# A late copy of row 0, a program order for POOL, k and x products in threes, and a first tile in quarters

## The chip, the cores and the metric

The kernel runs on one core of one Trainium2 chip. The metric is the device time in microseconds (us) of one execution; the time of a kernel is the median of eight executions.

## The reference, cut to what matters

The input x is 8 images of 256 channels of 96x96, in float32. Two residual layers follow each other, each on a group-normalised x (32 groups).

```
# layer 0: attention over channels on the 2D spectrum, 8 heads of 32 channels
q, k, v = [fft2(w @ gn(x) + b) for (w, b) in ((w1, b1), (w2, b2), (w3, b3))]
q, k    = q / norm(q), k / norm(k)                  # norms over all 96*96 frequencies
attn    = einsum('bhcn,bhdn->bhcd', q, k)
attn    = softmax(real(attn)) + 1j * softmax(imag(attn))
x       = x + w_out @ abs(ifft2(einsum('bhcd,bhdn->bhcn', attn, v)))
# layer 1: linear attention over positions; q and k have 32 rows, v has 256
q, k    = softplus(Wq @ gn(x) + bq), softplus(Wk @ gn(x) + bk)
v       = Wv @ gn(x) + bv
kv      = einsum('bdn,ben->bde', k, v)
x       = x + einsum('bnd,bde->ben', q, kv) / einsum('bnd,bd->bn', q, sum(k, over n) + 1e-6)
```

The kernel does no FFT of the image. It takes the attention from sums of products of an image with itself turned by 180 degrees, and from the turned image it makes the result in place.

## The kernel before, in words

An image is kept in SBUF as 128 partitions by 2 (the 256 channels) by 9216 columns. There are two such arenas; image b lies in one of them and its turned copy y in the other, which then takes the next image. A tile t is 8 rows of an image (12 tiles, loaded from t = 11 down to 0); `load_x` (L135) issues the loads of a tile on SP's queue, as two chunks of four rows.

Every image goes through five stages, each a Python generator:

- Pair sums (`pair_sums`, L325 on), 37 steps. A step takes 128 columns of x and the 128 opposite ones, which are turned back to the same order in `turn_back` (L364), one step ahead. In `turn_back`, at the first step of a tile, POOL first gathers the tile's column 0 in w0 (L371, L373 and, for t = 0, three smaller copies); then a copy from x, on POOL or ACT, writes the turned half to `back` (L387). PE transposes both halves in four matmuls each of 128x128 (L399, L400) into one PSUM tile, ACT scales and empties it into `xt` (L401), POOL (L414) or DVE (L416) form sum and difference in `eo`, and PE multiplies both with themselves into two accumulators (`products`, L333), one step later. From image 1 on the tiles t >= 5 are also spilled from xt to DRAM (L406, written xtd) for the next stage. Near the end of the stage the weights wl are loaded into a ring tile (L427).
- Attention (`attention`, L444 on): group norm, the covariances with the weights (L465), the softmax, with POOL's memsets L555 ahead of DVE's L558 and PE's product L561, and the matrix mz (POOL's memset L580).
- Rotation (`rotate`, L598 on): 48 steps of two rows each make the turned image y. `load_r` (L607) fetches a rotation matrix of six rows into a tm buffer, and POOL copies one column of it (L621). A step transposes two rows (PE L652, ACT L664) or fetches spilled ones from DRAM (L638, written xT<-xtd), and multiplies the rows of the step before last with tm (PE L655); DVE copies the result to ys (L660) and, turned, to y (L661). Row 0 has no partner and is copied as it is: POOL's copy L676 into y and memset L677 of ys, issued in the step where h is 0, step 6 of 48 (counted from 0). y lies in the arena of the image before, so its first writer waits until the outputs of that image have been stored.
- Images (`images`, L690 on): products with mz (L735), the squares and roots on DVE, ACT and POOL (L776 to L783), the product with w_out (L747), and x + result on DVE (L749). POOL sets two columns of the tiles of the next stage to 1.0 (L723).
- Layer 1 (`layer1`, L761 on) and its output (`output`, L949 on). Layer 1 works in 18 steps: PE transposes 512 columns of x in eight matmuls into two PSUM tiles (L893), ACT and DVE empty these into a slot (L896, L898), and `add_kx` (L871) multiplies a slot with the transposed k in eight matmuls with 32 columns of weights (L873). There are three slots. Two are in the constant tile xT and one is two tm buffers; a list `pend` holds the steps not yet multiplied, and products are issued for two steps together, just before the next step is appended. The softplus of k (DVE's L866 its last operation) and its transposes (PE L884, ACT L885) come once in three steps.

Buffers: psum has five rotating tiles for all transposes and products and three accumulators; the ring has four tiles of 128 x 1536 (xt, wl, own, e and others take turns); xT has six slots of 128 x 512, whose last two hold eo in the pair sums.

The stages are woven: `weave` advances one generator while another runs. The attention of image b runs beside its rotation; the pair sums of image b+1 run beside the images stage, layer 1 and output of image b. Where nothing else is said a scheduler orders each engine's instructions; within `tc.manual_schedule(engines=...)` the engines named keep the order in which the program issues them. That is PE around attention and rotation (L1025), and all five engines around the output stage (L1031 on), in which the generator of the next image's rotation is created but not yet run. POOL was free to be reordered in attention and rotation.

Of the kernel before, what the change touches and what calls it, by code (L numbers as in the profile page):

```python
# [62 lines left out]
TR = 6  # L63
# [9 lines left out]
def two_layer_kernel(ctx: ExitStack, tc: tile.TileContext, x, w1t, b1, w2t, b2, w3, b3, wot, temp,  # L73
                     wqt, bq, wkt, bk, wvt, bv, gavg, gmat, tmat, out):
    nc = tc.nc
    B, C, H, W = x.shape
    HW = H * W
    NT = H // ROWS
    TW = ROWS * W
    CH = 384  # L80
    PR = CH // W
# [18 lines left out]
    def x_of(b):  # L100
        return arenas[b % 2]
# [25 lines left out]
    def ring_tile(name):  # L127
        return ring.tile([P, 6 * C], F32, tag="ring", name=name)
# [5 lines left out]

    def load_x(b, t):  # L135
        loaded.add((b, t))
        for c in (2 * (NT - 1 - t), 2 * (NT - 1 - t) + 1):
            for h, n in chunk_rows(c):
                nc.sync.dma_start(out=x_of(b)[:, :, x_col(h):x_col(h) + n * W], in_=x_v[b, :, :, h * W:(h + n) * W])
# [185 lines left out]
    def pair_sums(b):  # L325
# [38 lines left out]
        def turn_back(i):  # L364

            t, j = steps[i]
            assert (b, t) in loaded
            if j == 0:
                col = x[:, :, (NT - 1 - t) * TW:(NT - t) * TW:W]
                h, o = PR * t, H // 2 + 1 + PR * t  # L370
                nc.gpsimd.tensor_copy(w0[:, :, h:h + PR], col[:, :, 0:PR])  # L371
                if t:
                    nc.gpsimd.tensor_copy(w0[:, :, o:o + PR], col[:, :, :PR - 1:-1])  # L373
                else:
                    nc.gpsimd.tensor_copy(w0[:, :, o:o + 1], col[:, :, 0:1])
                    nc.gpsimd.tensor_copy(w0[:, :, o + 1:o + PR], col[:, :, 2 * PR - 2:PR - 1:-1])
                    nc.gpsimd.tensor_copy(w0[:, :, o - 1:o], col[:, :, 2 * PR - 1:])
            if j == 0:
                xts.append(ring_tile(f"xt_{b}_{t}_{j}").rearrange("p (j c n) -> p j c n", j=3, c=2))
            ab = sides(t, j)  # L380
            ready = len(ab) == 1

            front = ab[0][2] if ready else xts[-1][:, j % 3, 0].rearrange("p (k n) -> p k n", k=KC)
            for p0, n, *v in ab:
                for c in range(ready, 2):
                    if v[c] is not None:
                        (nc.scalar.copy if b and t < T0 and (ready or not c) else nc.gpsimd.tensor_copy)(  # L387
                            (front, back[:, i % 2])[c][:, :, p0:p0 + n], v[c])
            return front, xts[-1][:, j % 3]

        steps = [(t, j) for t in range(NT - 1, -1, -1) for j in range(3)] + [(0, 3)]
# [206 lines left out]
    def rotate(b):  # L598

        y = image(y_of(b))  # L600
        ys = one.tile([P, KC, H + 1], F32, tag="ys", name=f"ys_{b}")

        def spilled(h):

            return b > 0 and PR * T0 <= h < H - PR * T0 and h != H // 2

        def load_r(h):  # L607
            tm = three.tile([P, TR * (W + 1)], F32, tag="tm", name=f"tm_{b}_{h}")[0:W].rearrange("p (r w) -> p r w", r=TR)
            turned = H // 2 <= h < H - PR * T0
            if b > turned:  # L610
                nc.sync.dma_start(out=tm, in_=rx[h // TR])
                return tm
            lo = 0
            while lo < TR:
                back = h + lo > H // 2 and spilled(h + lo)
                hi = lo + 2
                while hi < TR and back == (h + hi > H // 2 and spilled(h + hi)):
                    hi += 2
                nc.sync.dma_start(out=tm[:, lo:hi, 0:W], in_=window(h + lo, hi - lo, back))
                lo = hi  # L620
            nc.gpsimd.tensor_copy(tm[:, :, W:W + 1], csn[0:W, 2, h:h + TR].unsqueeze(2))  # L621
            if b == turned:
                nc.sync.dma_start(out=rx[h // TR], in_=tm)
            return tm


        pieces = [TR * i for i in (15, 4, 0, 5, 6, 14, 8, 3, 1, 7, 9, 13, 10, 12, 11, 2)]
        order = [h + r for h in pieces for r in range(0, TR, 2)]
        xts = {}

        def fetch(i):

            if i < len(order) and spilled(order[i]):
                xts[i] = xT[:, i % NX]
                h = order[i]
                c = h > H // 2
                rows = turned(c, H - h - 1 if c else h, 0)[0:2 * W]
                nc.sync.dma_start(out=xts[i][0:W, :, 0:C], in_=rows.rearrange("(r w) n -> w r n", w=W))  # L638

        def step(h, due, xt=None):  # L640

            if h is not None:
                pt = ps_tile(f"xr_{b}_{h}")
            if due is not None:
                g, gt, tm = due
                back = g > H // 2 and spilled(g)
                pu = ps_tile(f"y_{b}_{g}")
            for r in range(2):
                for k in range(KC):
                    if h is not None and h + r:  # L650
                        o = x_col(h + r)
                        nc.tensor.transpose(pt[0:W, r * C + k * P:r * C + (k + 1) * P], x_of(b)[:, k, o:o + W], ident)  # L652
                    if due is not None and g + r:
                        o = (r * KC + k) * (W + 1)
                        nc.tensor.matmul(pu[:, o:o + W + 1], lhsT=gt[0:W, 1 - r if back else r, k * P:(k + 1) * P], rhs=tm[:, g % TR + r, :],  # L655
                                         start=True, stop=True)
            if due is not None:
                src = pu[:, 0:2 * KC * (W + 1)].rearrange("p (r k w) -> p k w r", r=2, k=KC)
                r = 0 if g else 1
                nc.vector.tensor_copy(ys[:, :, g + r:g + 2], src[:, :, W, r:2])  # L660
                nc.vector.tensor_copy(y[:, :, :, g + r:g + 2], src[:, :, 0:W, r:2] if back else src[:, :, W - 1::-1, r:2])  # L661
            if h is not None:
                r = 0 if h else 1
                nc.scalar.copy(xt[0:W, r:2, 0:C], pt[0:W, r * C:2 * C].rearrange("p (r n) -> p r n", n=C))  # L664

        tms = [load_r(g) for g in pieces[0:3]]
        pieces = pieces[3:]
        pending = []
        for i, h in enumerate(order):
            if i % (TR // 2) == 0:  # L670
                tm = tms.pop(0)
            if i % (TR // 2) == 2 and i > 2 and pieces:
                tms.append(load_r(pieces.pop(0)))
            if h == 0:
                o = x_col(0)
                nc.gpsimd.tensor_copy(y[:, :, :, 0], x_of(b)[:, :, o:o + W])  # L676
                nc.gpsimd.memset(ys[:, :, 0:1], 0.0)  # L677
            if not spilled(h):
                xts[i] = xT[:, i % NX]
            step(None if spilled(h) else h, pending.pop(0) if len(pending) == 2 else None, xts[i])  # L680
            pending.append((h, xts.pop(i), tm))
            fetch(i + 3)
            yield
        for p in pending:
            step(None, p)
        y0[b] = ys
# [107 lines left out]
    def layer1(b):  # L794
# [78 lines left out]
                nc.tensor.matmul(kx[32 * j:32 * j + 32, 0:C + 1], lhsT=kT[:, 32 * j:32 * j + 32],  # L873
                                 rhs=xt[j // 2][:, j % 2, 0:C + 1], start=(i == 0), stop=(i == NS * CH // P - 1))

        slots = [*(xT[:, i] for i in range(4)), *kxt.pop(b)]
        pend = []
        softplus(0, 0)
        for s in range(NS):
# [4 lines left out]
                nc.tensor.transpose(pk[:, i * P:(i + 1) * P], kq(0, s)[:, i * P:(i + 1) * P], ident)  # L884
            nc.scalar.copy(kq(0, s), pk[:, 0:CH])  # L885
            for i in range(s * CH // P, (s + 1) * CH // P):
                xt = [slots[2 * (i % 3) + jj] for jj in range(2)]
                for jj in range(2):
                    pt = ps_tile(f"xT_{b}_{i}_{jj}")
                    for j in range(2):  # L890
                        o = (NB * s + 2 * jj + j) * CH + i % (CH // P) * P
                        for k in range(KC):
                            nc.tensor.transpose(pt[:, j * C + k * P:j * C + (k + 1) * P], x[:, k, o:o + P], ident)  # L893
                    src = pt.rearrange("p (j n) -> p j n", j=2)
                    if jj or i % 6 > 1:
                        nc.scalar.copy(xt[jj][:, :, 0:C], src)  # L896
                    else:
                        nc.vector.tensor_copy(xt[jj][:, :, 0:C], src)  # L898
                if s >= NS // 2 and i % (CH // P):
                    softplus(1, 2 * s - NS + i % (CH // P) - 1)  # L900
                if len(pend) == 2:
                    for p in pend:
                        add_kx(*p)
                    pend = []
                pend.append((i, xt, kq(0, s)[:, i % (CH // P) * P:(i % (CH // P) + 1) * P]))
                yield 0.25
# [115 lines left out]
        finish(sums)  # L1022
    turns = rotate(0)
    for b in range(B):
        with tc.manual_schedule(engines={mybir.EngineType.PE}):  # L1025
            weave(attention(b), turns)
            finish(turns)
        sums = pair_sums(b + 1) if b + 1 < B else iter(())
# [58 lines left out]
```

## Time and profile before

| | before |
|---|---|
| median of eight executions | 2731.66 us (2726.21 to 2749.8) |
| profiled execution | 2730.12 us |
| its span | 2728.3 us |
| mean granted clock of PE | 0.994 |
| PE's busy time | 2674.6 us (98%) |
| DVE, ACT, POOL | 1955.0, 1344.0, 884.8 us |
| HBM read, written | 151.25 MB, 118.06 MB |

The page gives the busy time of each engine over the span of one profiled execution, then the same in 40 slices of 68 us, with the granted clock of PE in tenths. The table of groups has one row for each line, engine and operation, with the mean duration of one instruction in ns and the idle time ahead of it, put down to the instruction that released it. The groups that the change touches:

```profile
L387 POOL COPY back<-arena 128x256 f32<-128x256 f32 (+1 forms) x230 | 89.6, 397 | 237.2 <-PE eoT L400 237.2
L400 PE MATMUL eoT<-ident,back 128*128 128x128 f32 x592 | 146.4, 274 | 1.8 <-POOL back L387 1.8
L676 POOL COPY arena<-arena 128x192 f32<-128x192 f32 x8 | 4.1, 510 | 25.4 <-DMA wl<-in_w_dram 11.8 <-DMA wl<-in_w2t_dram 6.5 <-DVE mv_a L295 3.4
L873 PE MATMUL kx<-xT,arena 128*32 128x257 f32 x768 | 56.3, 387 | 0.0
```

The timeline lists instructions by their start, with their duration, line, buffers and, in brackets, the idle time before them and who ended it.

### The profile page before, as it was taken

How to read it: one execution, taken by the hardware profiler on the slowest of the kernel's cores; microseconds unless marked ns; L12 is line 12 of the kernel's file. 1: busy time of each engine (PE TensorE's matmuls, PEld its weight loads, DVE VectorE, ACT ScalarE, POOL GpSimd, SP SyncE). 2: the span in 40 equal slices, each digit the busy share in tenths (PEclk: the TensorE clock that was granted, in tenths of full speed). 3: DMA queues.
4: the chain of work that ended last, by engine and by line, in shares of the span. 5: the costliest groups of instructions: out<-in, count | busy, mean ns of one | idle time of the engine just before them, and what ended most of it. 6: DMA issues, size and time to landing. Idle time of an engine off the chain costs nothing. (4 is left out here: it accounts for less than half of the span.)

```text
span 2728.3 us, 47818 instructions
## 1 busy us (share of the span) xinstructions
PE 2674.6 (98%) x17606; PEld 1915.0 (70%) x17606; DVE 1955.0 (72%) x4218; ACT 1344.0 (49%) x2125; POOL 884.8 (32%) x1334
## 2 busy tenths in 40 slices
PE   8999999999999999999999999999999999999987
PEld 8965678656785577956778566785677856778555
DVE  6678576875768767687666875768657687577776
ACT  3455653556525564255642556425564355643554
POOL 6133431334403334044340442404424134141311
PEclk9999999999999999999999999999999999999998
DMA  5220156202652026420364203641036311362003
GB/s 175 67 68 12 62 200 187 72 7 74 218 149 68 9 84 221 129 70 15 104 209 116 68 22 98 217 119 55 26 105 224 109 47 36 102 221 82 1 7 139
DMA packets 228635, 272.43 MB, mean 100 GB/s; under 512 B 34154, under 2 KB 216596, under 8 KB 228404
## 3 DMA queue, kind: packets, MB, share of 16 engines
q1 hardware_dynamic: 227460, 269.04, 31.3%
q8 instruction: 141, 2.31, 0.4%
q14 instruction: 90, 0.74, 0.1%
q10 hardware_dynamic: 944, 0.34, 0.0%
HBM read 151.25 MB, written 118.06 MB: 99 GB/s over the span
## 5 line engine op out<-in xcount | busy, mean ns | idle before, releaser
L735 PE MATMUL z<-arena,mz 128*128 128x384 f32 (+2 forms) x2400 | 595.0, 476 | 0.0
L747 PE MATMUL po<-e,wo 128*128 128x384 f32 x1536 | 529.8, 486 | 0.2 <-ACT e L782 0.2
L781 POOL TENSOR_TENSOR e<-e 128x768 f32<-128x768 f32 x192 | 348.6, 1816 | 554.0 <-ACT e L780 553.4
L735 PEld LDWEIGHTS z<-arena,mz 128*128 128x128 f32 (+1 forms) x2400 | 325.6, 163 | 241.4 <-issue 42.4
L333 PE MATMUL acc<-xT 128*128 128x256 f32 (+1 forms) x2368 | 449.1, 330 | 16.7 <-POOL xT L414 15.7
L747 PEld LDWEIGHTS po<-e,wo 128*128 128x128 f32 x1536 | 289.5, 190 | 197.7 <-DVE arena L749 1.2
L776 DVE TENSOR_TENSOR e<-z,xT 128x768 f32<-128x768 f32 x384 | 365.7, 952 | 85.2 <-PE z L735 85.1
L333 PEld LDWEIGHTS acc<-xT 128*128 128x128 f32 x2368 | 382.4, 191 | 60.2 <-POOL xT L414 21.2
L286 DVE BATCH_NORM_STATS2 st<-arena 128x6 f32<-128x384 f32 x768 | 409.7, 553 | 15.8 <-DMA arena<-in_x_dram 5.7
L655 PE MATMUL y<-tm,xT 96*128 96x97 f32 x3040 | 411.1, 269 | 1.6 <-DMA xT<-xtd 0.9
L655 PEld LDWEIGHTS y<-tm,xT 96*128 96x128 f32 x3040 | 402.1, 192 | 13.1 <-issue 7.4
L780 ACT ACTIVATE e<-e 128x1536 f32<-128x1536 f32 x192 | 284.5, 1482 | 91.4 <-DVE e L776 89.9
L782 ACT ACTIVATE e<-e 128x768 f32<-128x768 f32 x192 | 162.0, 844 | 336.7 <-POOL e L781 335.7
L401 ACT ACTIVATE xt<-eoT,pw 128x512 f32<-128x512 f32 x296 | 203.5, 687 | 163.7 <-PE eoT L400 153.7
L749 DVE TENSOR_TENSOR arena<-arena,po 128x384 f32<-128x384 f32 x384 | 211.0, 551 | 92.5 <-PE po L747 68.6
L414 POOL TENSOR_TENSOR xT<-xt 128x256 f32<-128x256 f32 x352 | 257.0, 747 | 60.4 <-ACT xt L401 59.3
L664 ACT COPY xT<-xr 96x512 f32<-96x512 f32 (+1 forms) x195 | 111.3, 574 | 276.4 <-PE xr L652 275.8
L661 DVE COPY arena<-y 128x384 f32<-128x384 f32 (+1 forms) x384 | 208.6, 546 | 2.0 <-issue 0.9
L652 PE MATMUL xr<-ident,arena 128*96 128x128 f32 x764 | 200.9, 279 | 0.0
L387 POOL COPY back<-arena 128x256 f32<-128x256 f32 (+1 forms) x230 | 89.6, 397 | 237.2 <-PE eoT L400 237.2
L988 DVE TENSOR_TENSOR arena<-arena,o 128x384 f32<-128x384 f32 x288 | 142.0, 549 | 33.8 <-PE o L983 33.8
L416 DVE SCALAR_TENSOR_TENSOR xT<-eoT,pw,xt 128x256 f32<-128x256 f32 x240 | 107.1, 478 | 81.9 <-ACT xt L401 81.9
(228 smaller groups left out, 3201.4 us busy)
## 6 DMA issues: line engine op xcount, KB each, us to landing
arena<-in_x_dram SPq DMA_DIRECT2D x184, 384.0 KB
out_dram<-arena SPq DMA_DIRECT2D x184, 384.0 KB
xT<-xtd SPq DMA_DIRECT2D x189, 192.0 KB
xtd<-xt SPq DMA_DIRECT2D x196, 128.0 KB
tm<-rx SPq DMA_DIRECT2D x107, 218.2 KB
xtd<-xt SPq DMA_DIRECT2D x98, 127.0 KB
rx<-tm SPq DMA_DIRECT2D x16, 218.2 KB
tm<-rt SPq DMA_DIRECT2D x16, 216.0 KB
```

The source lines that it names most:

```text
L286: nc.vector.bn_stats(out=st[:, k, c, :], in_=x_of(b)[:, k, c * CH:(c + 1) * CH])
L333: mm = nc.tensor.matmul(acc[c][:, m * C:m * C + (KC - m) * P], lhsT=t[0:np_, c, m * P:(m + 1) * P], rhs=t[0:np_, c, m * P:C], start=(first ...
L401: nc.scalar.activation(both, pt, AF.Copy, scale=pw[:, j:j + 1])
L414: on_pool(eo[:, c], both[:, 0], both[:, 1])
L655: nc.tensor.matmul(pu[:, o:o + W + 1], lhsT=gt[0:W, 1 - r if back else r, k * P:(k + 1) * P], rhs=tm[:, g % TR + r, :], start=True, stop=True)
L661: nc.vector.tensor_copy(y[:, :, :, g + r:g + 2], src[:, :, 0:W, r:2] if back else src[:, :, W - 1::-1, r:2])
L735: mm = nc.tensor.matmul(out[:, o:o + n * W], lhsT=columns(mz, k, c, j), rhs=y[:, k, h * W:(h + n) * W], start=(k == 0 and o == 0), stop=(k ...
L747: nc.tensor.matmul(po[:, 0:CH], lhsT=wo[:, k, m * P:(m + 1) * P], rhs=e[:, k, :], start=(k == 0), stop=(k == KC - 1))
L749: nc.vector.tensor_add(x[:, m, n], x[:, m, n], po[:, 0:CH])
L776: nc.vector.tensor_add(e[:, 2 * c:2 * c + 2, :].rearrange("p t (q h) -> p t q h", h=H), pz[:, 0:CH].rearrange("p (q h) -> p q h", h=H).uns ...
L780: nc.scalar.activation(e, e, AF.Square)
L781: nc.gpsimd.tensor_add(e[:, 0:2, :], e[:, 0:2, :], e[:, 2:4, :])
```

## The change

It has five edits.

1. `load_x`: the first tile of image 0 is loaded in four DMAs of two rows instead of two of four. The order of the rows is 44, 51, 46, 49 (the first row of each), so that opposite rows follow each other.
2. `turn_back`: the copies L387 are issued ahead of the copies of column 0 to w0 (L371 on).
3. `rotate`: row 0's copy and the memset of ys are issued at step 42 of 48 (counted from 0), right after the last rotation matrix has been fetched, instead of in the step where h is 0.
4. `layer1`: a fourth slot, `kring`, is taken from the ring, with a memset of its columns of 1.0 on POOL. Products are issued for three steps together.
5. The manual schedule around attention and rotation holds POOL as well as PE.

```diff
 def load_x(b, t):
     loaded.add((b, t))
+    if (b, t) == (0, NT - 1):
+        for h in (H // 2 - PR, H // 2 + PR - 1, H // 2 - 2, H // 2 + 1):
+            nc.sync.dma_start(out=x_of(b)[:, :, x_col(h):x_col(h) + 2 * W], in_=x_v[b, :, :, h * W:(h + 2) * W])
+        return
...
         if j == 0:
+            xts.append(ring_tile(f"xt_{b}_{t}_{j}").rearrange("p (j c n) -> p j c n", j=3, c=2))
+        ab = sides(t, j)
+        ready = len(ab) == 1
+
+        front = ab[0][2] if ready else xts[-1][:, j % 3, 0].rearrange("p (k n) -> p k n", k=KC)
+        for p0, n, *v in ab:
...
+        if j == 0:
             col = x[:, :, (NT - 1 - t) * TW:(NT - t) * TW:W]
...
-        if j == 0:
-            xts.append(ring_tile(f"xt_{b}_{t}_{j}").rearrange("p (j c n) -> p j c n", j=3, c=2))
-        ab = sides(t, j)
-        ready = len(ab) == 1
...
-        if h == 0:
+        if i == len(order) - TR:
             o = x_col(0)
             nc.gpsimd.tensor_copy(y[:, :, :, 0], x_of(b)[:, :, o:o + W])
             nc.gpsimd.memset(ys[:, :, 0:1], 0.0)
...
-    slots = [*(xT[:, i] for i in range(4)), *kxt.pop(b)]
+    kring = ring_tile(f"kx_{b}")[:, 0:4 * (C + 2)].rearrange("p (i j n) -> p i j n", i=2, j=2)
+    nc.gpsimd.memset(kring[:, :, :, C:C + 2], 1.0)
+    slots = [*(xT[:, i] for i in range(4)), *kxt.pop(b), *(kring[:, i] for i in range(2))]
...
-            xt = [slots[2 * (i % 3) + jj] for jj in range(2)]
+            xt = [slots[2 * (i % 4) + jj] for jj in range(2)]
...
-            if len(pend) == 2:
+            if len(pend) == 3:
...
-    with tc.manual_schedule(engines={mybir.EngineType.PE}):
+    with tc.manual_schedule(engines={mybir.EngineType.PE, mybir.EngineType.Pool}):
         weave(attention(b), turns)
         finish(turns)
```

More of the change, by code (lines that the diff above doesn't have):

```diff
@@ L368, in turn_back @@
             if j == 0:
+                xts.append(ring_tile(f"xt_{b}_{t}_{j}").rearrange("p (j c n) -> p j c n", j=3, c=2))
[3 more added lines that the diff above has]
+            for p0, n, *v in ab:
+                for c in range(ready, 2):
+                    if v[c] is not None:
+                        (nc.scalar.copy if b and t < T0 and (ready or not c) else nc.gpsimd.tensor_copy)(
+                            (front, back[:, i % 2])[c][:, :, p0:p0 + n], v[c])
+            if j == 0:
                 col = x[:, :, (NT - 1 - t) * TW:(NT - t) * TW:W]
@@ L377, in turn_back @@
                     nc.gpsimd.tensor_copy(w0[:, :, o - 1:o], col[:, :, 2 * PR - 1:])
-            if j == 0:
-                xts.append(ring_tile(f"xt_{b}_{t}_{j}").rearrange("p (j c n) -> p j c n", j=3, c=2))
-            ab = sides(t, j)
-            ready = len(ab) == 1
[L383 to L388, printed above, removed]
             return front, xts[-1][:, j % 3]
```

## The prediction

> **What bounds the kernel now.** I read the page's busy times and slices first, then who PE waited for, then the timelines at the longest of those waits.
>
> ```profile
> PE 2674.6 (98%) x17606; PEld 1915.0 (70%) x17606; DVE 1955.0 (72%) x4218; ACT 1344.0 (49%) x2125; POOL 884.8 (32%) x1334
> PE   8999999999999999999999999999999999999987
> PEclk9999999999999999999999999999999999999998
> ```
>
> PE is busy 98% of the 2728.3 us span, in every slice, at nearly full granted clock. So only two things shorten this kernel: removing PE's waits (some 54 us idle, plus what the clock loses after a wait), or making PE's own sequence cheaper. Time saved on POOL, DVE or ACT counts only where PE waits for it. The waits of PE:
>
> ```profile
> engine line waited for: us in total, times, longest us
> PE acc L333 <- POOL xT L414: 15.7, 14, 3.2
> PE kT L884 <- DVE arena L866: 6.2, 8, 3.6
> ```
>
> The first row is the largest: the pair-sum products L333 wait for POOL's subtraction L414. The timeline shows where, at the end of image 1's pair sums; POOL first, then PE:
>
> ```profile
> 414.85 0.73 POOL L414 TENSOR_TENSOR xT<-xt 128x256 f32<-128x256 f32 x1 [0.50 <-ACT xt L401]
> 415.51 0.10 POOL L677 MEMSET ys<- 128x2 f32 x1
> 419.23 0.51 POOL L676 COPY arena<-arena 128x192 f32<-128x192 f32 x1 [3.61 <-DMA wl<-in_w_dram]
> 419.61 0.72 POOL L414 TENSOR_TENSOR xT<-xt 128x256 f32<-128x256 f32 x1
> ```
>
> ```profile
> 415.82 2.43 PE L333 MATMUL acc<-xT 128*128 128x256 f32 x12
> 420.39 0.92 PE L333 MATMUL acc<-xT 128*128 128x256 f32 x4 [2.14 <-POOL xT L414]
> 421.15 1.04 PE L652 MATMUL xr<-ident,arena 128*96 128x128 f32 x8
> ```
>
> L414's input (ACT's L401) is ready at 416.76. It starts at 419.61 because row 0's copy L676 stands ahead of it on POOL and waits 3.61 us until the buffer it writes has been stored; the DMA named is merely the last to land by then. The same picture is there for images 1 to 7. Image 0's copy stands elsewhere (35.60) and PE does not wait for it.
>
> **What the Trainium skill says.** "PSUM — Partial Sum Buffer", section "Engine vs sequencer instructions", calls GpSimd's queue strict FIFO. The trace agrees: L414 with its input ready for 2.8 us stays behind L676. "TensorE: Matmul & The Clock Gate", section "What's actually happening", says that about 3.4 us of idle window bring half clock until a busy window has passed. The trace agrees in part: the granted clock is 0.50 in 757.8 to 761.2 and 1761.3 to 1764.7, right after two of these waits, though they last only 3.23 and 1.95 us. "TensorEngine Tiling (Array Packing)", section "Key Properties", says that changing the tiling mode drains TensorE; the kx products are 128x32 tiles between 128x128 transposes, and their cost at the change is measured below. "DMA: Bandwidth & Descriptors", section "Queues, rings and completion order", says that each DMA engine takes a ring's descriptors in order. The trace agrees: the first x tile's first half is there at 4.71, its second at 6.01.
>
> **Part 1: row 0's copy later, POOL in program order.** In the changed program's built order the copy and its memset stand behind the last of the copies L621 (image 0, 1) or the memset L580, after both last L414s. So in images 1 to 7 L414 follows L401: 416.76, plus 0.1 and 0.72, gives 417.6. PE finishes twelve products at 418.0 (415.82 plus eight and four at their usual pace, with 0.2 for DVE's L416), so no wait is left. Image 0 does the same sixteen in 73.22 to 76.14, 2.92 us. From the first to the transpose behind them, images 1 to 7 take 5.33, 6.42, 5.16, 4.83, 5.83, 5.12 and 4.42 us: 37.1, less 7 x 2.92 = 20.4, leaves **16.7**. The half clock also slows what follows: from that transpose to the qkm product (L465) it is 6.56 us in image 1, 8.18 in image 2 and 7.39 in image 5: **2.4** more. Sum 19.1.
>
> What is late next: DVE's first copy into that buffer (L661) waits for the same stores. It runs at 424.22; 2.4 earlier is 421.8, and L676 was released at 419.2, so 2.6 us of margin. The spilled rows (xT<-xtd) are issued from 417.16 on; their first product falls at about 425.5 now, 423.1 then, and the transfers queued before them drain at about 421.5 by the DMA packets: 1.5 us margin. The weights wl are needed only at 427.7.
>
> The copy itself, 0.51 us on POOL some six steps before the rotation ends, and the memset lie under PE's rotation; uncovered they would cost 8 x 0.6 = 5 us. Program order also puts the softmax memsets L555 behind some L621, which wait for PE to free a tm buffer; DVE's L558, then PE's L561, stand behind. Image 0 is the tightest: L558 at 116.58 moves behind the L621 of 117.63, about 1.5 us later; L561 comes at 126.24, so nothing reaches PE. L580 leaves the output stage, where POOL waited up to 4.9 us on it, but PE had no wait there: nothing.
>
> **Part 2: products of k and x for three steps together.** The timeline of PE around a group of two steps (each step is 8 records):
>
> ```profile
> 336.43 0.64 PE L873 MATMUL kx<-xt,arena 128*32 128x257 f32 x8
> 336.89 0.62 PE L873 MATMUL kx<-xT,arena 128*32 128x257 f32 x8
> 337.44 1.09 PE L893 MATMUL xT<-ident,arena 128*128 128x128 f32 x8
> 343.34 1.04 PE L893 MATMUL xT<-ident,arena 128*128 128x128 f32 x8
> 344.31 1.07 PE L873 MATMUL kx<-xT,arena 128*32 128x257 f32 x16
> 345.31 0.55 PE L884 MATMUL kT<-ident,arena 128*128 128x128 f32 x3
> ```
>
> Start to start, a step takes 0.46 inside a group and 0.55 as its last: leaving costs 0.09. Eight transposes take 0.97 before a group (343.34 to 344.31), against 0.87 elsewhere (332.85 to 333.72): entering costs 0.10. 18 steps in groups of three are six groups instead of nine: 3 x 0.19 = 0.57 us an image, 4.6 for eight. Against it: ahead of the first group PE now makes ten transposed tiles in a row instead of seven, through five PSUM buffers. Step 1's tiles are emptied at 331.84 by ACT and DVE; PE would want their buffers at about 331.6, so some 0.25 us an image goes back. Net 0.32 x 8 = **2.6**; bounds 4.6 gained and, if 0.15 us is lost at each of 48 groups, 2.6 lost.
>
> The fourth slot is a ring tile, so the pair sums have two tiles left beside it and own. The memset adds a wait on POOL: it needs xt_9's spill to have landed, and behind it are L414 of t = 7 and the products. That spill is issued by 311.8, the memset comes at about 325: nothing, as for the other tiles (xt_6 at 342.3 follows xt_8's spill, issued by 324.1; xt_5 at 364.6 that of xt_7, issued by 337.6). On SP, xt_6's last spill falls behind the tm loads, some 5 us later; xt_3, which takes its buffer, starts after 375.
>
> **Part 3: first tile in quarters, back copies first.** POOL's start now:
>
> ```profile
> 4.71 0.19 POOL L371 COPY w<-arena 128x8 f32<-128x8 f32 x1 [0.93 <-DMA arena<-in_x_dram]
> 6.01 0.19 POOL L373 COPY w<-arena 128x8 f32<-128x8 f32 x1 [1.10 <-DMA arena<-in_x_dram]
> 6.14 0.74 POOL L387 COPY back<-arena 128x256 f32<-128x256 f32 x2
> ```
>
> The first step needs the first two quarters, the bytes of the first half: at 4.7 instead of 6.0. POOL then copies back at once, and PE's first step ends about 1.4 us sooner. But the next step needs the last quarter, still near 6.0, and PE's fourth and fifth transposes need tile 10, which two more issues of 0.46 us on SP ahead of 23 loads push back. The trace has no transfer of this size, so bounds: 1.6 gained (the lead kept) to 0.5 lost (the issues dominate). I take **1.0**. In later images the copies L387 before L371 save POOL 0.4 us where PE does not wait.
>
> **Sum.** 19.1 + 2.6 + 1.0 = 22.7. The profiled execution took 2730.12 (span 2728.3 and 1.8 around it) and would take 2707.4; the median of the eight runs is 1.54 higher: 2731.66 - 22.7 = **2709.0**.
>
> **Rivals.** *Late rows* (0.12): PE reaches the spilled rows while stores, weights and they share the DMA engines. For: such a wait exists once (1.13 us at 477.8). Against: the 1.5 us margin. 7 x 1.1 = 7.7 back: 2716.7. *The wait moves* (0.05): DVE's L661 takes over L676's wait, so PE stops one step later and only 3.6 is gained: 2728.1. For: the same stores are awaited. Against: 2.6 us margin. *Slower* (0.05): PE waits for PSUM at each group of three, because ACT needs 5 x 0.59 + 0.48 + 0.62 = 4.1 us to empty what PE makes in 2.95. Without the 2.6, parts 1 and 3 give 20.1: it decides from 20.1/48 = 0.42 us a group. At 0.7 it costs 33.6, ending at 2745. Against: ACT is busy 26.1 of 35 us in this stage, and product blocks of 1.3 us lie between.
>
> **Chances and range.** The likeliest case has 0.78, 2709.0. Its own bounds: 2705 (all of part 2, 1.6 of part 3) to 2717 (part 2 losing, part 3 losing 0.5, and 1.3 of clock loss staying), with 4 us of run to run spread: 2700 to 2720, which takes in late rows. A measurement of this kernel tells about 0.3%, 8.2 us, from no change. Faster by more 0.90 (0.78 + 0.12), within 0.05, slower 0.05.
>
> **What would show it.** The row of L333 waiting for L414 falls from 15.7 to about 3; no half clock after the pair sums; kx records in runs of 24; PE's first L400 near 5.3 instead of 6.59. Wrong if y L655 waits for xT<-xtd in every image, if L661's idle grows, or if PE's transposes L893 wait for ACT's L896.

## The result, and the profile after

| | before | after |
|---|---|---|
| median | 2733.44 us (32 executions, 2725.89 to 2749.8) | 2719.39 us (11 executions, 2715.08 to 2723.72) |
| ratio after / before | | 0.9945, 95% interval 0.9929 to 0.9960 |
| profiled execution: span | 2728.3 us | 2716.3 us |

The kernel is 0.55% faster: 14.0 us by the medians, 10.9 to 19.4 by the interval. The forecast was 22.7 us. The line numbers of the changed kernel are 4 to 6 higher behind `load_x` (L414 is now L418, L676 is L680); in `turn_back`, turned round, L387 is now L381 and L371 is L386. First the page's busy times, PE's slices and its clock, after the change:

```profile
PE 2670.3 (98%) x17606; PEld 1911.7 (70%) x17606; DVE 1957.6 (72%) x4218; ACT 1342.6 (49%) x2125; POOL 884.0 (33%) x1342
PE   8999999999999999999999999999999999999987
PEclk9999999999999999999999999999999999999999
```

At this size nothing can be seen. The waits of PE show the difference (line, who is waited for, us in total, times, longest):

```profile
PE kT L890 <- DVE arena L870: 6.2, 8, 3.6
PE eoT L403 <- DMA arena<-in_x_dram: 5.2, 2, 3.9
PE xT L899 <- ACT xT L902: 2.8, 7, 0.4
PE zs L704 <- DVE ys L664: 2.8, 8, 0.3
PE acc L337 <- POOL xT L418: 1.8, 8, 0.3
```

The 15.7 us of the products on POOL's subtraction are 1.8. Two rows have come: the transposes of layer 1 wait for ACT's L902 once in seven of the eight images, and the first transposes wait a second time for x. The timeline of POOL at the end of image 1's pair sums, and later in its rotation:

```profile
417.06 0.74 POOL L418 TENSOR_TENSOR xT<-xt 128x256 f32<-128x256 f32 x1 [0.50 <-ACT xt L405]
419.11 0.73 POOL L418 TENSOR_TENSOR xT<-xt 128x256 f32<-128x256 f32 x1 [1.31 <-ACT xt L405]
...
472.36 0.19 POOL L625 COPY tm<-csn 96x6 f32<-96x6 f32 x1 [4.58 <-DMA xT<-xtd]
472.48 0.53 POOL L680 COPY arena<-arena 128x192 f32<-128x192 f32 x1
472.86 0.15 POOL L681 MEMSET ys<- 128x2 f32 x1
```

Nothing stands between the last two subtractions any more; POOL only waits for ACT, whose output it reads. Row 0's copy comes 53 us later and waits for nothing. PE at the same place and, further up in the same timeline, around layer 1's third group:

```profile
346.38 0.60 PE L899 MATMUL xT<-ident,arena 128*128 128x128 f32 x4
347.39 0.63 PE L899 MATMUL xT<-ident,arena 128*128 128x128 f32 x4 [0.41 <-ACT xT L902]
347.95 0.64 PE L877 MATMUL kx<-xt,arena 128*32 128x257 f32 x8
348.41 0.62 PE L877 MATMUL kx<-kx,arena 128*32 128x257 f32 x8
348.84 0.62 PE L877 MATMUL kx<-xT,arena 128*32 128x257 f32 x8
...
418.03 3.08 PE L337 MATMUL acc<-xT 128*128 128x256 f32 x16
420.95 1.04 PE L656 MATMUL xr<-ident,arena 128*96 128x128 f32 x8
```

The sixteen last products run through: 2.92 us from the first to the transpose behind them, where it was 5.33. The third group of kx products is now 24 records, and ahead of it PE stops for 0.41 us in the middle of a step's transposes.

To split the difference I cut the spans at starts of PE records: zs (L700), kT (L884) and den (L936) of each image, by the numbers of before. The way from den to the next zs holds the output, the end of the pair sums, attention and rotation; from kT to den lie the 18 steps of layer 1.

| stretch | before | after | difference |
|---|---|---|---|
| start to zs of image 0 | 150.25 | 152.05 | +1.80 |
| den to zs, images 1 to 7 | 825.42 | 808.17 | -17.25 |
| kT to den, images 0 to 6 | 273.76 | 276.46 | +2.70 |
| layer 1 of image 7 up to kT | 24.99 | 26.41 | +1.42 |
| den of image 7 to the end | 38.19 | 37.65 | -0.54 |

With the rest, -0.2, this is the 12.0 us between the spans. The 1.42 has no part of the change in it: after the same waits, PE's clock was granted at half for 6.8 us in the execution after and for 3.4 in the one before. Most of the 1.80 at the start is no part of the change either: PE's clock is full from 13.61 us on in the execution after, and from 10.28 in the one before. In the ten kernels below that load the first tile in halves, zs of image 0 comes about 0.5 us later for each us that the full clock comes later (10.28 and 150.25 us before, 13.11 and 151.69 in the last kernel of the table below); by this estimate 1.7 of the 1.80 are the clock's.

### The profile page after: what moved, and what is told of

Its sections match the earlier page's. It is cut to its first block, busy times and chain, and to the rows that moved or that the text cites. A ratio compares the mean times of both kernels' runs of the same rounds, so it can differ in the third digit from the quotient of the medians.

```text
span 2716.3 us, 47888 instructions
## 1 busy us (share of the span) xinstructions
PE 2670.3 (98%) x17606; PEld 1911.7 (70%) x17606; DVE 1957.6 (72%) x4218; ACT 1342.6 (49%) x2125; POOL 884.0 (33%) x1342
## 5 line engine op out<-in xcount | busy, mean ns | idle before, releaser
L405 ACT ACTIVATE xt<-eoT,pw 128x512 f32<-128x512 f32 x296 | 203.6, 688 | 173.2 <-PE eoT L404 161.6
L418 POOL TENSOR_TENSOR xT<-xt 128x256 f32<-128x256 f32 x352 | 257.0, 747 | 71.1 <-ACT xt L405 65.6
L998 POOL TENSOR_TENSOR arena<-arena,po 128x384 f32<-128x384 f32 x96 | 96.4, 1004 | 229.1 <-ACT po L997 226.7
L381 POOL COPY back<-arena 128x256 f32<-128x256 f32 (+1 forms) x230 | 85.8, 379 | 253.2 <-PE eoT L404 243.0
```

The lines of the kernel that those rows point to most:

```text
L405: nc.scalar.activation(both, pt, AF.Copy, scale=pw[:, j:j + 1])
L418: on_pool(eo[:, c], both[:, 0], both[:, 1])
```

## The experiments

Each kernel has the edits shown and otherwise is the kernel before, or the changed one where that is said. The table cuts one profiled execution of each as above. A median and a ratio are given where several executions were timed; the other kernels have one execution. "Half clock" counts the stretches from den to zs of images 1 to 7 with half granted clock in them; "last 16" is the sum over them of the time from the first of the last sixteen products to the transpose behind; "rows" is PE's wait for spilled rows (y <- DMA xT<-xtd).

| kernel | span | den to zs | half clock | last 16 | rows | kT to den, mean | first product |
|---|---|---|---|---|---|---|---|
| before | 2728.3 | 825.4 | 2 | 37.1 | 0.9 | 39.11 | 9.69 |
| changed | 2716.3 | 808.2 | 0 | 20.4 | 0.4 | 39.49 | 10.08 |
| row and POOL order | 2718.3 | 811.8 | 1 | 20.4 | 2.2 | 39.11 | 9.88 |
| row only | 2750.9 | 844.6 | 3 | 38.1 | 0.2 | 39.11 | 9.56 |
| POOL order only | 2732.6 | 829.5 | 3 | 35.8 | 0.2 | 39.11 | 9.63 |
| threes only | 2747.2 | 841.0 | 5 | 36.6 | 0.6 | 39.57 | 9.65 |
| first tile only | 2730.4 | 824.2 | 1 | 36.1 | 0.9 | 39.11 | 9.30 |
| quarters only | 2735.2 | 827.1 | 3 | 37.8 | 0.8 | 39.11 | 11.70 |
| row, POOL, back first | 2717.6 | 815.3 | 2 | 20.4 | 3.6 | 39.11 | 9.66 |
| changed, no threes | 2717.6 | 811.0 | 0 | 20.4 | 3.6 | 39.11 | 9.32 |
| row, POOL, fourth slot, twos | 2715.4 | 810.4 | 0 | 20.4 | 2.7 | 39.03 | 9.86 |
| row, POOL, last three | 2721.8 | 816.3 | 0 | 20.4 | 3.0 | 39.53 | 9.68 |
| row, POOL, twos, no q softplus | 2746.5 | 810.2 | 0 | 20.4 | 2.4 | 39.08 | 9.78 |
| row, POOL, threes, no q softplus | 2731.7 | 812.0 | 0 | 20.4 | 1.3 | 38.09 | 9.65 |

**Row 0's copy and the POOL order, together and apart.**

```diff
-            if h == 0:
+            if i == len(order) - TR:
...
-        with tc.manual_schedule(engines={mybir.EngineType.PE}):
+        with tc.manual_schedule(engines={mybir.EngineType.PE, mybir.EngineType.Pool}):
```

Both edits:

> The kernel before with only row 0's copy at step 42 and POOL in program order. Theory: this part carries the whole gain. In the two traces the way from den (PE L936) to zs (L700) is shorter in images 1 to 7 by 2.17, 4.87, 2.26, 1.64, 3.77, 1.93 and 1.27 us, 17.9 in all, so this kernel is 17.9 us faster than before, and its row of L333 waiting for L414 is near 2 us. Rival: the measured gain of all parts together (about 14 us by the medians) is this part's own gain, something else in its stages is lost and the other parts cost nothing: 14 us faster.

Measured: median 2718.6 us, ratio 0.9920 (0.9890 to 0.9951), 13 to 30 us faster. The last sixteen take 2.92 us in each image. The ratio holds the 17.9 of the theory and the 14 of the rival alike; that this part carries the gain is shown by the next two and by the stretches. First the first line of the diff alone, then the last alone:

> The kernel before with only row 0's copy at step 42; POOL is still free in attention. Theory: the scheduler puts the copy by what it expects of its inputs, not by where the program issues it, and in the built order it still stands ahead of the last L414. So nothing changes: L333 waits about 15 us for L414, den to zs takes 116.5 to 120 us in images 1 to 7, no gain. Rival: the place in the program decides alone, the wait falls to about 2 us and the kernel gains 16 to 18 us without the POOL order.

> The kernel before with only POOL in program order; row 0's copy stays in the step where h is 0. Theory: in the built order the copy stands right ahead of the last L414 from image 1 on, as before, and only in image 0 behind it; L333 still waits about 15 us and the kernel gains nothing. Rival: program order alone is enough, the wait falls to about 2 us, 16 to 18 us faster.

Measured: neither takes the wait away. The row of waits, with the row's place alone and with the POOL order alone:

```profile
PE acc L333 <- POOL xT L414: 16.8, 14, 3.1
```

```profile
PE acc L333 <- POOL xT L414: 14.4, 16, 2.1
```

With the place alone the scheduler, free on POOL, puts the copy where it was (in image 1 L676 starts at 419.82, L414 behind it at 420.21). With the program order alone the program itself issues it ahead of the last subtraction (419.25 and 419.67). Only both together move it: the gain belongs to the pair.

**The threes.**

```diff
-        slots = [*(xT[:, i] for i in range(4)), *kxt.pop(b)]
+        kring = ring_tile(f"kx_{b}")[:, 0:4 * (C + 2)].rearrange("p (i j n) -> p i j n", i=2, j=2)
+        nc.gpsimd.memset(kring[:, :, :, C:C + 2], 1.0)
+        slots = [*(xT[:, i] for i in range(4)), *kxt.pop(b), *(kring[:, i] for i in range(2))]
...
-                xt = [slots[2 * (i % 3) + jj] for jj in range(2)]
+                xt = [slots[2 * (i % 4) + jj] for jj in range(2)]
...
-                if len(pend) == 2:
+                if len(pend) == 3:
```

> The kernel before with only the fourth slot and products of k and x for three steps. Theory: the longer rows of transposes wait for PSUM tiles that ACT and DVE empty late, so each image's way from the first kT (L890 after) to den (L942) is 39.5 us instead of 39.1, and the kernel is 0.44 x 7 = 3 us slower. Rival, the step as predicted: fewer changes of tile size win, 2.6 us faster, and the loss seen in the changed kernel comes from the other parts.

Measured: median 2748.37 us, ratio 1.0043 (1.0025 to 1.0062), 7 to 17 us slower, more than either theory said. Layer 1 costs what the theory said, 39.57 for 39.11 (3.2 us in seven images). The rest is in the stretches from den to zs, which this edit leaves alone: five of seven had half clock after the wait for L414, two of them for 13.7 us. One of those, by windows (us, then each engine's busy time, then the granted clock ahead of the DMA share):

```profile
1775.00:1788.00 13.00, 13.00 (x64) 11.50 (x62) 5.31 (x21) 3.71 (x7) 0.00 (x0) 0.50 0.23 62
```

PE issues 64 matmuls in these 13 us; the changed kernel issues 97 in 13 us at about this point. Why the threes alone bring more half clock than the kernel before is open: the last sixteen take 36.6 us in all, no more than the 37.1 before. The profile is no outlier: 22 executions lay between 2732.5 and 2765.0.

Next, on top of the row and POOL order, the fourth slot and its memset as above, but with `len(pend) == 2` kept.

> Row 0's copy and the POOL order of the change, with the fourth slot from the ring and its memset, but products for two steps together. Theory: grouping costs, not the slot: kT to den takes 39.1 us an image, as with three slots. Rival: the ring tile, its memset or the pair sums' shorter ring cost: 39.5 us, as with the threes.

Measured: 39.03 us, so the slot costs nothing in this stage and the grouping does. Next, whether the wait is for PSUM tiles that ACT and DVE empty late. Both kernels have the row and POOL order and leave out the softplus of q; one has twos and three slots, the other the threes above.

```diff
-                if s >= NS // 2 and i % (CH // P):
-                    softplus(1, 2 * s - NS + i % (CH // P) - 1)
```

> Row 0's copy and the POOL order of the change, three slots, groups of two, without the softplus of q (five DVE and ACT operations in each of six rounds are left out, q stays without its softplus). To be compared with the same in threes. Theory: with groups of two PE is not held up in this stage, so leaving out the work saves nothing, or at most the 0.4 of the last group: kT to den stays at 38.7 to 39.1 us.

> As the run before, without the softplus of q, but with the fourth slot and products for three steps. Theory: the threes lose because ACT and DVE, busy with the softplus of q, empty the transposed tiles late (waits of 0.57 and 0.28 us an image in the second half of the steps); without that work these waits go, and the threes show the 0.55 us of three fewer groups: kT to den is shorter than with twos by 0.3 to 0.6 us. Rival: the waits come from the five PSUM tiles alone, or from how the steps of the pair sums are interleaved, and the threes stay 0.4 us longer than the twos.

Measured: twos 39.08, threes 38.09, 0.99 shorter. The wait for ACT in the third group is gone. PE issues the same 377 instructions in the same order from kT to den as in the changed kernel, so that only its waits differ. So with ACT and DVE relieved the threes pay, and with the softplus of q there they cost. In the changed kernel this is ACT ahead of the copies L902 for which PE stops at 347.39:

```profile
344.66 0.61 ACT L868 ACTIVATE spu<-spu,own 128x384 f32<-128x384 f32 x1 [0.59 <-DVE arena L867]
345.64 0.69 ACT L405 ACTIVATE xt<-eoT,pw 128x512 f32<-128x512 f32 x1
346.23 1.07 ACT L902 COPY xT<-xT 128x512 f32<-128x512 f32 x2
```

L868 belongs to the softplus, L405 to the pair sums. (As whole kernels the two are slower than the row and POOL order alone. Between the start of layer 1 and kT the images took 284 and 279 us instead of 253, with waits of the pair sums' transposes for ACT: the scheduler had arranged that stretch otherwise.)

0.99 is more than the 0.3 to 0.6 expected. 0.4 of it comes from the last group. First the row and POOL order in twos without q's softplus, then the changed kernel, PE at the last products of the step loop:

```profile
1042.43 0.64 PE L873 MATMUL kx<-xT,arena 128*32 128x257 f32 x8
1042.89 1.02 PE L873 MATMUL kx<-xt,arena 128*32 128x257 f32 x8
1043.84 0.33 PE L399 MATMUL eoT<-ident,arena 128*128 128x128 f32 x1
```

```profile
364.58 0.64 PE L877 MATMUL kx<-kx,arena 128*32 128x257 f32 x8
365.04 1.07 PE L877 MATMUL kx<-xT,arena 128*32 128x257 f32 x16
366.04 0.33 PE L403 MATMUL eoT<-ident,arena 128*128 128x128 f32 x1
```

In twos the last step takes 0.95 us instead of 0.55, since its operands have just been transposed; with two steps ahead of it (365.04 to 366.04 for the last two, 1.0 in all) it does not wait. I tried to take this 0.4 without the rest: one step, seven times two, then three, with three slots, on the row and POOL order.

```diff
-                if len(pend) == 2:
+                if i < 17 and len(pend) == (2 if i > 1 else 1):
```

> Row 0's copy and the POOL order of the change, three slots, products for one step, then seven times two, and three at the end. Theory: in the kernel before the last group has only one step's products (0.46 us) to cover the copies of the last step, and takes 1.41 us instead of 1.0; with two steps ahead it does not wait: 0.4 us an image less (38.7 from kT to den), 3 us in all, at the same number of groups. It then is near 2715 us, 19 us faster than before. Rival: the other phase of the groups against the softplus makes the same PSUM waits as the threes, and it is level with or above the row and POOL order alone (2718.6).

Measured: median 2729.44 us, ratio 0.9974 (0.9961 to 0.9986), only 4 to 11 us faster than before. That is the rival's outcome: 39.53 us from kT to den. Its mechanism, PSUM waits like those of the threes, is not what the new waits show:

```profile
PE rec L953 <- ACT xt L434: 4.1, 7, 0.6
...
PE kx L873 <- ACT spu L864: 3.0, 7, 0.4
```

The first is in the output stage. The second is at the first group, in seven of the eight images: the products of its only step stop for 0.43 us and then take 1.05 us instead of 0.55, because ACT copies half of that step's own tiles only at 331.38 (image 0), behind a softplus of k. The last group did get shorter by 0.4, since its three steps take 1.47 us where the last two took 1.41 in twos. So a group of one step loses at the start more than is won at the end. The scatter of this kernel is not accounted for: 22 executions lie between 2722.6 and 2742.9.

**The first tile.**

```diff
+        if (b, t) == (0, NT - 1):
+            for h in (H // 2 - PR, H // 2 + PR - 1, H // 2 - 2, H // 2 + 1):
+                nc.sync.dma_start(out=x_of(b)[:, :, x_col(h):x_col(h) + 2 * W], in_=x_v[b, :, :, h * W:(h + 2) * W])
+            return
```

With this and the back copies L387 ahead of the column copies:

> The kernel before with only the first tile in quarters and the back copies first. Theory: the third quarter lands late (PE waited for it until 7.35 us in the changed kernel), zs of image 0 starts at 151.4 us instead of 149.7, 1.7 slower. Rival, the step as predicted: 1.0 faster (148.7), the loss at the start of the changed kernel being one of the other parts' (the moved memset L580, or the other place of row 0's copy in image 0).

With the quarters alone:

> The kernel before with only the first tile in quarters; the column copies still stand ahead of the back copies. Theory: the quarters bring the first step about 0.8 us sooner, but the third quarter lands no sooner than the second half did, and with the column copies waiting for the whole tile ahead of the back copy the first step's second operand is later still: the first product of the pair sums is not earlier than before (9.69 us), rather 0.5 to 1.5 later. Rival, as predicted for both edits together: 0.5 to 1.6 us earlier.

Measured: both edits, first product at 9.30 us, zs at 150.54; quarters alone, 11.70 and 152.43. Neither size was met. With the quarters alone POOL shows why (start, duration):

```profile
7.33 0.19 POOL L375 COPY w<-arena 128x8 f32<-128x8 f32 x1 [3.55 <-DMA arena<-in_x_dram]
8.03 0.19 POOL L377 COPY w<-arena 128x8 f32<-128x8 f32 x1 [0.50 <-DMA arena<-in_x_dram]
8.15 0.73 POOL L391 COPY back<-arena 128x256 f32<-128x256 f32 x2
```

The third quarter is there at 7.33 and the fourth at 8.03, where the second half was there at 6.01. With the back copies first, PE in the changed kernel:

```profile
3.91 0.45 PE L403 MATMUL eoT<-ident,arena 128*128 128x128 f32 x1 [3.91 <-DMA arena<-in_x_dram]
5.15 0.47 PE L404 MATMUL eoT<-ident,back 128*128 128x128 f32 x1 [0.80 <-POOL back L381]
...
7.35 0.47 PE L403 MATMUL eoT<-ident,arena 128*128 128x128 f32 x1 [1.29 <-DMA arena<-in_x_dram]
8.54 0.48 PE L404 MATMUL eoT<-ident,back 128*128 128x128 f32 x1 [0.72 <-POOL back L381]
```

The first step is over 1.4 us sooner (5.15 instead of 6.59), and the second waits. The three kernels with both edits have their first product at 9.30, 9.32 and 10.08, the ten kernels with halves at 9.56 to 9.88.

**Without the parts that cost.** The changed kernel without threes and quarters, then without threes only:

```diff
-                xt = [slots[2 * (i % 4) + jj] for jj in range(2)]
+                xt = [slots[2 * (i % 3) + jj] for jj in range(2)]
...
-                if len(pend) == 3:
+                if len(pend) == 2:
```

The fourth slot and its memset go too.

> The changed kernel without its threes (three slots, groups of two) and without the quarters: the row and POOL order, and the back copies first, are left. Theory: it keeps the 17.9 us and loses neither the 3 us of layer 1 nor the 1.7 at the start, and the back copies first give up to 1 us at the start: 17.9 to 18.9 us faster than before, some 4 us faster than the changed kernel. Rival: the parts do not add up, and it is level with the changed kernel, 14 us faster than before.

> The changed kernel with three slots and groups of two; all else as changed. Theory: 39.07 us from kT to den in each image instead of 39.5, 2.7 us off the changed kernel, some 17 us faster than before; the third quarter's landing sets the start, the waits until the second step adding up to 6 to 7 us. Rival: the threes pay elsewhere, by bringing the spilled rows earlier than PE needs them, and the time is that of the changed kernel or above (13 us faster than before), with more waits of y for xT<-xtd.

Measured: 2718.25 us, ratio 0.9917 (0.9882 to 0.9952), and 2718.52 us, ratio 0.9944 (0.9927 to 0.9960). Neither can be told from the changed kernel. Without the threes kT to den is 39.11 again, 2.7 us less in all, but PE waits 3.6 us for spilled rows where the changed kernel's profile has 0.4: in part the rival. All eight kernels without the wait for L414 have such waits, 0.4 to 3.6 us, and the other threes there (without q's softplus) 1.3, so that the threes bring rows sooner is not shown. I found no version that beats the changed kernel beyond the noise.

## Why the prediction was right, and where it was not

Direction, range and main cause held; the gain was over-estimated by 8.7 us of 22.7. Luck had a part in the range: 2719.39 is 0.6 us inside its end, and beyond 2717, the bound of the likeliest case. (2705, its other bound, was counted from the profiled execution; from the median, as 2717 was, it is 2706.4.) Between the two profiles the gain is 12.0, and the 10.7 that are missing are 1.9 in part 1, 5.3 in part 2, 2.8 at the start, which is mostly the clock, and 0.7 in the rest.

- **L333's wait, 16.7 us.** The size and the mechanism were right: 37.1 us of last sixteens became 20.4, 2.92 in each image, in all eight kernels with both edits.
- **Half clock after it, 2.4.** The mechanism was right and the size depends on the execution. In the two profiles shown two stretches with half clock became none. Over all profiles, 17 of 42 stretches with the wait have it, and 3 of 56 without. The cost of one is not constant: "row only" has 124.2 to 125.9 us in the three stretches with 13.7 or 17.1 us of half clock, and 117.0 to 118.4 in the other four. Executions with a lower granted clock tend to be the longer ones: of the kernel before, one took 2727.71 us at a mean of 0.993 and one 2767.25 at 0.979. So half clock after the wait is a part of the scatter of the kernels that have it, 2726 to 2767 us, against 9 us of the changed one. It is not the only source: "row, POOL, last three" scatters over 20 us without the wait.
- **What is late next.** The step said that the spilled rows have 1.5 us of margin and nothing comes back. This failed in part: in the kernels with both edits PE waited 0.4 to 3.6 us for them, against 0.2 to 0.9 in those with the wait left. The row and POOL order alone shows the worst one, 4 us after the place where L414's wait was:

```profile
422.79 2.00 PE L655 MATMUL y<-tm,xT 96*128 96x97 f32 x16
426.42 2.85 PE L655 MATMUL y<-tm,xT 96*128 96x97 f32 x12 [1.63 <-DMA xT<-xtd]
```

  The rival "late rows" had the right mechanism. The waits alone are less than half of its price (7.7), but all three half-clock stretches without the wait for L414 come with a stop like this one (1.30 to 1.63 us), and this loss is larger: in "row, POOL, back first" images 5 and 6 have such a stop and take 119.79 and 118.25 us from den to zs, and image 7, without one, 115.10. That is 7.8 us for the two. zs also waits 0.7 us longer in all for DVE's L660. The rival "the wait moves" is not borne out: DVE's L661 idles 1.4 us in all after, and 1.8 before.
- **Part 2, 2.6 gained.** Wrong in sign: 2.7 lost over seven images. The loss was put at 0.25 an image, the wait for PSUM ahead of the first group, and this much the threes lose without q's softplus too (0.06, 0.09 and 0.10 us around that group). The gain was put at 0.57; with 0.99 net it is 1.24, of which 0.4 lie in the last group, which I had not seen. Of the other 0.27 a part is the middle step of a group, which takes 0.43 us (348.41 to 348.84) and not 0.46; the rest is open. With q's softplus the same threes take 39.49 instead of 38.09, 1.40 more: 0.57 in the third group, some 0.75 around the fifth, 0.07 ahead of the second. The failed step is the one that costed the first group and took it for all: in the second half of the steps ACT and DVE have the softplus of q and the pair sums' copies ahead of the PSUM copies in their queues. The rival "slower" named the mechanism at 0.7 us a group; it is (0.25 + 1.40) / 6 = 0.28. That ACT is busy 26.1 of 35 us was no argument against it, since the wait comes from the order of its work at one place. The sign of error that the prediction named, PE's transposes L893 waiting for ACT's L896, is in the profile after.
- **Part 3, 1.0 gained.** About nothing: in the three kernels with both edits the first product is 0.4 later to 0.4 earlier than before, and zs of image 0, less 0.5 us for each us of late clock, 0.1 later to 0.4 earlier. The term that failed is "the next step needs the last quarter, still near 6.0": the third quarter alone held PE until 6.43 and 7.35 in two of these kernels and was there at about 6.4 in the other, and the last came at 7.1 to 8.0. Beside the quarters the back copies first were worth more than assumed: without them the first product comes 2.0 us later than before. Beside halves they show no gain (9.66 against 9.56 to 9.88). The start differs by more than that between kernels (zs at 150.25 to 152.43) because the clock becomes full anywhere from 10.3 to 13.6 us. This agrees with the Trainium skill, "TensorE: Matmul & The Clock Gate", section "What's actually happening": the window that decides on the clock runs free of the kernel's start. What the page says of recovery, full clock after one busy window of about 3.4 us, is not what the 13 us at 0.50 shown above agree with: by the profile's records, whose ends are modelled, PE was busy all through them.

## What to carry to other kernels

The wait on POOL's queue went only when both were right, the place in the program and the rule that orders the queue; test the two apart before crediting either. Grouping work to spare switches asked more of the engines that empty the buffers, and it cost most at the busiest group and not at the first: cost each group with what stands in ACT's and DVE's queues there. When a first load is split, look at when the last piece that the second step needs arrives, and not only at the first.

## What the runs showed of the hardware that was not expected

Half clock came with stops of PE of 1.3 to 3.2 us in an otherwise full stream, but not after each: 17 of the 42 stretches with the wait for L414 have it. In these stretches it lasted 3.4, 6.8, 13.7 or 17.1 us, whole multiples of 3.41.

A tile loaded in four transfers of two rows (768 bytes a packet) had its third piece there at 6.4 to 7.35 us and its last at 7.1 to 8.0, in four kernels. In two transfers of four rows (1536 bytes a packet) the whole tile is there at 5.9 to 6.2, in ten kernels, though the bytes and the queue are the same. By 7 us the queue had moved 1.10 MB in the changed kernel and 1.31 MB before. Whether the packets, the two more issues or the loads of ACT's queue beside them make the difference was not separated.
